# Sign convolutions with two output channels in one float32r weight, layer 1 by row pairs, and attention without the row maximum

## The chip, the core and the metric

The kernel runs on one core of a Trainium2 chip. Five engines work side by side and wait for one another through semaphores: TensorE (PE: matmuls, and PEld: the loads of their weights), VectorE (DVE), ScalarE (ACT), GpSimd (POOL) and SyncE (SP), which here only starts transfers. The metric is the device time of one execution in microseconds. Three runs of the kernel before gave 2253.57, 2254.1 and 2255.21 us; the profiled execution spans 2262.4 us.

## The reference

The input is 16 images of 256 channels and 28 x 28 pixels. Four layers follow each other.

- Layer 0: `sign(x)` is convolved (3x3, 256 to 256 channels) with `sign(w)`; the sum, times the mean of |w| per output channel, goes through a batch norm over all images and is added to x.
- Layer 1: `sign(x)` is convolved 3x3 with float32 weights clipped to -1..1; a fixed affine map, a parametric ReLU, a gate (two tiny dense layers on channel means, with ReLU and sigmoid), a product with the residual and another affine map follow. A second branch does the same with a 1x1 convolution.
- Layer 2: batch norm over all images, sign, sign convolution, parametric ReLU; batch norm, sign, sign convolution, parametric ReLU; batch norm, plus the input, parametric ReLU.
- Layer 3: attention over the 784 pixels of each image with 64 reduced channels:

```python
q = jnp.einsum('rc,bcn->bnr', Wq, xf)
k = jnp.einsum('rc,bcn->brn', Wk, xf)
v = jnp.einsum('rc,bcn->bnr', Wv, xf)
attn = jax.nn.softmax(jnp.einsum('bnr,brm->bnm', q, k) * scale, axis=-1)
out = jnp.einsum('cr,brn->bcn', Wp, jnp.einsum('bnm,bmr->brn', attn, v))
return out.reshape(B, C, H, W) + x
```

A batch norm over all images needs the statistics of every image before the next sign can be taken, so the work falls into stages: layer 0, layer 1, the first and the second convolution of layer 2, attention.

## The kernel before

Channels lie on the 128 partitions in two halves (`k` for input, `mo` for output), the 784 pixels of an image on the free axis. Each stage loops over the 16 images. A scheduler orders each engine's instructions from the program's order and the data dependencies; rotating buffers of the pools decide how far an image may run ahead.

A 3x3 convolution (`conv3x3`, L137) is 18 matmuls (two halves of input channels, nine taps) for each half of the output channels and each half image `h` (14 rows, 392 columns, one PSUM bank), accumulated in PSUM. Signs and sign weights are bfloat16: 72 matmuls an image for layer 0 (L243) and for each convolution of layer 2 (`conv2`, L441). In layer 1 the float32 weights are split into three bfloat16 parts (`split3`, L128), so the convolution takes 216 matmuls an image (L400, L418), and the 1x1 convolution (`conv1x1`, L364) 24.

Around the convolutions: in layer 0 ACT takes signs into a padded image (L212) and copies the integer sums to int16 tiles `y0` (L244), while DVE collects statistics (L246); y0, and later x2 in the same pool, stay in SBUF for all 16 images. In layer 1, `enter` (L297) makes x1, its signs and the residual; `bn_prelu` (L315) turns a PSUM sum into y; `gate_hidden` and `gate` compute the gates, and `branch1` and `branch2` (L350, L382) apply them one and two images later. In layer 2 `prelu_n` (L182) and the statistics (L448) are DVE's and the copy to int16 (L446) ACT's.

Attention works on chunks of 112 rows (`MC`), seven to an image. For each image `row_max` (L537) computes the scores chunk by chunk and reduces each to a row maximum on DVE; `put_max` (L550) transposes the maxima into an extra row of q, so that a second score product (`attend`, L569) comes out with the maximum subtracted; ACT takes the exponential (L574); another product with v sums the values, and, as 64 columns of v are ones, the denominators too (L581). DVE takes the reciprocal of the denominators (L586) and multiplies (L587). `project` (L590) multiplies with Wp and adds x. While image b is attended, `qkv(b + 1)` (L517) and `project(b - 1)` are put between its steps. All matmuls of attention are float32.

Of the kernel before, what the change touches and what calls it, by code (L numbers as in the profile page):

```python
"""conv_seq d4 on 16x256x28x28: binary conv + BN, two-branch SE block, binary conv x2 + BN, attention.

Layout: channels on partitions (two halves of 128), pixels (784) on the free axis, one tile per
image.  Activations that are signs (-1, 0, 1) and sign weights are held in bfloat16, and
convolution sums of signs (integers of magnitude <= 2304) in int16: both hold them exactly.  The
float32 weights that meet sign activations (layer 1) are split into three bfloat16 parts whose sum
is the float32 weight, so that these products are exact too; everything else is float32.

Algebra used: stop_gradient(a - b) + b is a; sums of 2304 signs never reach the saturation of layer
0; the mean of s*x + (1-s)*y is taken from the two means; a per-channel constant of layer 1's output  # L10
is carried along (`cc`) into layer 2's last bias, as layer 2's first batch norm doesn't see it.
"""
# [10 lines left out]
BF = mybir.dt.bfloat16  # L23
I16 = mybir.dt.int16
AF = mybir.ActivationFunctionType
# [7 lines left out]
N = S * S          # pixels of an image  # L33
HN = N // 2        # half an image: one matmul, one PSUM bank
HR = S // 2
K9 = 256 * 9
MC = 112           # attention rows per chunk
# [3 lines left out]
#: The per-channel vectors, in the order of their columns.  # L41
# [10 lines left out]
def conv_seq_kernel(ctx: ExitStack, tc: tile.TileContext, d: dict, out: bass.AP):  # L52
# [6 lines left out]
    xr = ctx.enter_context(tc.tile_pool(name="xr", bufs=B))  # L59

# [9 lines left out]

    pads = [const.tile([P, 2, S + 2, S + 2], BF, tag=f"pad{i}", name=f"pad{i}") for i in range(2)]
    for p in pads:
        nc.gpsimd.memset(p, 0.0)

# [7 lines left out]
    def inv_std(name, var):  # L82
        """1 / sqrt(var + EPS) of a [P, 2] tile, the square root's table corrected by a Newton step."""
        v, r, t = vtile(name + "_v"), vtile(name + "_r"), vtile(name + "_t")
        V.tensor_scalar(v, var, EPS, None, ALU.add)
        A.activation(t, v, AF.Sqrt)
        V.reciprocal(r, t)
        tt(t, r, r, ALU.mult)
        tt(t, t, v, ALU.mult)
        V.tensor_scalar(t, t, -0.5, 1.5, ALU.mult, ALU.add)  # L90
        return tt(r, r, t, ALU.mult)

    def affine(name, inv, gamma, beta, mean):
        """scale = gamma * inv and bias = beta - mean * scale."""
        s, c = vtile(name + "_s"), vtile(name + "_c")
        tt(s, gamma, inv, ALU.mult)
        tt(c, mean, s, ALU.mult)
        tt(c, beta, c, ALU.subtract)
        return s, c

# [1 line left out]
    def load_taps(pool, src, k, g):  # L102
        st = pool.tile([P, 3, 256], F32, tag="st", name="st", bufs=2)
        nc.sync.dma_start(out=st, in_=src[k, :, 3 * g:3 * g + 3, :])
        return st

    def sign_chunk(pool, dst, src, acc, k, g):
        """Three taps of sign(w) into dst, and their part of sum |w| in PSUM, [P, 2]."""
        st = load_taps(pool, src, k, g)
        A.activation(dst[:, k, 3 * g:3 * g + 3, :], st, AF.Sign)  # L110
        ab = pool.tile([P, 256], F32, tag="ab", name="ab", bufs=2)
        V.tensor_reduce(ab, st.rearrange("p t o -> p o t"), AX.X, ALU.add, apply_absolute_value=True)
        part = acc.tile([P, 2], F32, tag="sm", name="sumabs")
        for mo in range(2):
            T.matmul(part[:, mo:mo + 1], lhsT=ab[:, mo * P:(mo + 1) * P], rhs=ones, start=True, stop=True)
        return part

    def sign_weights(pool, dst, src, total, acc):
        """A list of steps: dst = sign(w), total = mean |w| per output channel."""
        def step(k, g):  # L120
            part = sign_chunk(pool, dst, src, acc, k, g)
# [4 lines left out]
        return [lambda k=k, g=g: step(k, g) for k in range(2) for g in range(3)]  # L126

    def split3(dsts, st):  # L128
        """clip(w, -1, 1) as the sum of three bfloat16 tiles."""
        V.tensor_scalar(st, st, -1.0, 1.0, ALU.max, ALU.min)  # L130
        A.copy(dsts[0], st)
        tt(st, st, dsts[0], ALU.subtract)
        A.copy(dsts[1], st)
        tt(st, st, dsts[1], ALU.subtract)
        A.copy(dsts[2], st)

    def conv3x3(ps, pad, wts, mo):  # L137
        """ps[:, h, :HN] = 3x3 convolution of the padded image, output channels of half mo."""
        n, last = 0, len(wts) * 18 - 1
        for w in wts:  # L140
            for k in range(2):
                for t in range(9):
                    r, c = divmod(t, 3)
                    for h in range(2):
                        T.matmul(  # L145
                            ps[:, h, :HN].rearrange("p (a b) -> p a b", b=S),
                            lhsT=w[:, k, t, mo * P:(mo + 1) * P],
                            rhs=pad[:, k, r + h * HR:r + h * HR + HR, c:c + S],
                            start=(n == 0),
                            stop=(n == last),  # L150
                        )
                    n += 1

    def inner(pad, k):
        return pad[:, k, 1:S + 1, 1:S + 1]
# [4 lines left out]
    def halves(ap):  # L160
        return ap.rearrange("p (h n) -> p h n", h=2)

    def mean_var(name, st):
        """Per-channel mean and variance from [P, 2, chunks, 6] statistics."""
# [8 lines left out]
    def sign_bn(name, sf, m, v, gamma, beta):  # L173
        """Batch norm of sf * n from the mean and variance of n: scale and bias for n."""
# [7 lines left out]
    def prelu_n(pool, n, alpha, bufs=2):  # L182
        """Parametric ReLU of the integers n (SBUF or PSUM, [P, 2, HN]) in float32."""
        t = pool.tile([P, 2, HN], F32, tag="t", name="t", bufs=bufs)
        p = pool.tile([P, 2, HN], F32, tag="p", name="p", bufs=bufs)
        V.tensor_scalar(t, n, 0.0, alpha, ALU.min, ALU.mult)  # L186
        V.scalar_tensor_tensor(p, n, 0.0, t, ALU.max, ALU.add)  # L187
        return p

    stats_x2 = const.tile([P, 2, 2 * B, 6], F32, name="stats_x2")  # L190
    stats = const.tile([P, 2, 2 * B, 6], F32, name="stats")
    sf0, sf1, sf2 = vtile("sf0"), vtile("sf1"), vtile("sf2")
    w0 = wpool.tile([P, 2, 9, 256], BF, tag="wa", name="w0")

    x2 = [None] * B
    with tc.tile_pool(name="ps_conv", bufs=3, space=PSUM) as psc, \
# [4 lines left out]

        with tc.tile_pool(name="ph1", bufs=1) as ph:
            # ======== layer 0: sign(x) * sign(w), kept as integers, with their statistics ========
            xs = [None] * B

            def load_x(b):
                xs[b] = ph.tile([P, 2, N], F32, tag="xs", name=f"xs{b}", bufs=3)
                nc.sync.dma_start(out=xs[b], in_=d["x"][b])

            def sign0(b):  # L210
                for k in range(2):
                    A.activation(inner(pads[b % 2], k), img(xs[b][:, k, :]), AF.Sign)  # L212

            steps = sign_weights(ph, w0, d["w0"], sf0, pss)
            load_x(0)
            sign0(0)
            for s in steps:
                s()
            load_x(1)

            w1 = [ph.tile([P, 2, 9, 256], BF, name=f"w1_{i}") for i in range(3)]
            fw = [ph.tile([P, 2, 256], BF, name=f"fw_{i}") for i in range(3)]

            def w1_step(k, g):
                st = load_taps(ph, d["w1"], k, g)
                split3([w[:, k, 3 * g:3 * g + 3, :] for w in w1], st)

            def fw_step():
                st = ph.tile([P, 3, 256], F32, tag="st", name="stf", bufs=2)
                nc.sync.dma_start(out=st[:, 0:2, :], in_=d["fw"])  # L230
                split3(fw, st[:, 0:2, :])

            steps = [lambda k=k, g=g: w1_step(k, g) for k in range(2) for g in range(3)] + [fw_step]
            y0 = [None] * B
            for b in range(B):
# [4 lines left out]
                y0[b] = xr.tile([P, 2, N], I16, tag="xr", name=f"y0_{b}")  # L240
                for mo in range(2):
                    ps = conv_ps()
                    conv3x3(ps, pads[b % 2], [w0], mo)  # L243
                    A.copy(halves(y0[b][:, mo, :]), ps[:, :, :HN])  # L244
                    for h in range(2):
                        V.bn_stats(stats[:, mo, 2 * b + h, :], ps[:, h, :HN])  # L246
                if b >= 2 and steps:
                    steps.pop(0)()
            load_x(0)
            load_x(1)  # L250

            # ======== layer 1 ========
            # Constants of the layer, [P, 2] each.
# [6 lines left out]
            def mix(name, scale, shift):  # L260
                """mean(s * (x + shift) + (1 - s) * y) = sum(x) * a + sum(y) * b + c."""
# [411 lines left out]
```

## Time and profile before

The page gives the busy time of each engine over the span of 2262.4 us, in which busy stretches of different engines overlap.

| what | value |
|---|---|
| time, median of three | 2254.1 us |
| TensorE busy | 2126.3 us, 94% |
| VectorE busy | 1041.2 us, 46% |
| ScalarE busy | 496.2 us, 22% |
| layer 0, first to last matmul | 12 to 209 us |
| layer 1 | 222 to 932 us |
| layer 2, first and second convolution | 933 to 1133 and 1143 to 1342 us |
| attention | 1358 to 2262 us |

A group of instructions is listed as line, engine, operation, output and input with their sizes, count; then busy time and mean duration of one; then the idle time of the engine just before them and what ended it. Matmuls are pipelined: the mean of one is longer than the distance between two. The granted clock is TensorE's, 1.0 being full.

### The profile page before, as it was taken

To read this page: it belongs to the slowest core of one execution; us is meant where nothing else is said; L and a number is where in the kernel's file an instruction comes from. 1 tells how busy PE (TensorE), PEld (TensorE's weight loads), DVE (VectorE), ACT (ScalarE), POOL (GpSimd) and SP (SyncE) were. 2 spreads that over 40 slices of the span, in tenths; PEclk is the share of its full clock that TensorE was granted. 3 is DMA by queue.
4 is the path that set the end of the run, shared out by engine and by line. 5 is a ranking of instruction groups with operands and counts; after the bars stand their busy time and mean duration, and the time that the engine had idled before them with its cause. 6 is when DMAs were issued, how large, how long until landed. Compare 5 with 4: busy or idle time off the path is not lost.

```text
span 2262.4 us, 22710 instructions
## 1 busy us (share of the span) xinstructions
PE 2126.3 (94%) x9896; PEld 1170.4 (52%) x9896; DVE 1041.2 (46%) x1628; ACT 496.2 (22%) x659; POOL 6.5 (0%) x13
## 2 busy tenths in 40 slices
PE   8998999999999998699989979999999999999997
PEld 4554555555555555355545544444444444444443
DVE  5213244454454454554567765677653233222232
ACT  5322122122122111323222321222211111111111
POOL 0000000000000000000000000000000000000000
PEclk9999999999999999799999985688778777777776
DMA  5221000000000000100000000000000000000000
GB/s 204 73 72 43 1 29 29 15 29 15 15 29 15 15 15 1 42 1 1 1 1 1 1 5 1 14 14 15 14 14 15 14 15 14 14 14 14 15 15 28
DMA packets 11603, 50.11 MB, mean 22 GB/s; under 512 B 1776, under 2 KB 2160, under 8 KB 11504
## 3 DMA queue, kind: packets, MB, share of 16 engines
q1 hardware_dynamic: 11504, 48.67, 6.2%
q8 instruction: 77, 1.26, 0.2%
q14 instruction: 22, 0.18, 0.0%
HBM read 35.82 MB, written 12.85 MB: 22 GB/s over the span
## 4 chain that ended last, share of the span: by engine, by line
PE 90%; DVE 8%; ACT 1%; issue 0%; DMA 0%; SPq 0%; ACTq 0%
PE cv L145 53%; PE sc L543 10%; PE sc L569 7%; PE av L581 6%; PE mi L594 4%; DVE r L586 4%; PE cv L372 3%; PE mi L522 3%; PE mi L531 2%; PE av L554 2%; PE gate L343 1%; DVE nm L547 1%; DVE p L187 1%; DVE x L515 0%; DVE t L186 0%; DVE x L511 0%
## 5 line engine op out<-in xcount | busy, mean ns | idle before, releaser
L145 PE MATMUL cv<-pad,w 128*128 128x392 bf16 x4608 | 799.4, 333 | 8.7 <-ACT pad L305 8.7
L145 PEld LDWEIGHTS <-w 128*128 128x128 bf16 x4608 | 445.0, 97 | 343.6 <-issue 12.2
L543 PE MATMUL sc<-qk 64*112 64x392 f32 x448 | 263.8, 764 | 51.6 <-DVE nm L547 51.6
L543 PEld LDWEIGHTS sc<-qk 64*112 64x112 f32 x448 | 116.3, 267 | 186.9 <-issue 116.9
L145 PE MATMUL cv<-pad,w2b 128*128 128x392 bf16 x1152 | 198.3, 334 | 11.1 <-ACT pad L465 11.1
L569 PE MATMUL sc<-qk 65*112 65x392 f32 x448 | 202.8, 575 | 0.0
L145 PE MATMUL cv<-pad,w2a 128*128 128x392 bf16 x1152 | 198.3, 333 | 2.4 <-ACT pad L436 2.4
L294 DVE TENSOR_SCALAR t<-sy,vec 128x784 f32<-128x784 f32 x32 | 20.1, 628 | 340.7 <-ACT sy L318 340.7
L581 PE MATMUL av<-es,va 112*128 112x392 f32 x448 | 170.2, 509 | 1.6 <-ACT es L574 1.6
L586 DVE RECIPROCAL r<-av 64x784 f32<-64x784 f32 x16 | 80.9, 5057 | 190.3 <-PE av L581 190.3
L547 DVE TENSOR_REDUCE nm<-sc 112x1 f32<-112x784 f32 x112 | 108.9, 972 | 121.2 <-PE sc L543 120.8
L145 PEld LDWEIGHTS <-w2b 128*128 128x128 bf16 x1152 | 111.9, 97 | 97.5 <-issue 13.6
L145 PEld LDWEIGHTS <-w2a 128*128 128x128 bf16 x1152 | 112.2, 98 | 87.3 <-issue 3.9
L186 DVE TENSOR_SCALAR t<-cv,vec 128x784 f32<-128x784 f32 x64 | 66.2, 1034 | 158.6 <-PE cv L145 158.6
L574 ACT ACTIVATE es<-sc 112x784 f32<-112x784 f32 x112 | 91.9, 823 | 205.3 <-PE sc L569 205.2
L569 PEld LDWEIGHTS sc<-qk 65*112 65x112 f32 x448 | 85.7, 202 | 82.9 <-issue 71.5
L581 PEld LDWEIGHTS av<-es,va 112*128 112x128 f32 x448 | 87.7, 196 | 69.4 <-issue 18.7
L446 ACT CAST n<-cv 128x784 int16<-128x784 f32 x64 | 52.0, 812 | 229.3 <-DVE p L187 229.3
L318 ACT ACTIVATE sy<-cv,abn_c,abn_s 128x784 f32<-128x784 f32 x32 | 32.1, 1003 | 315.4 <-PE cv L145 315.4
L594 PE MATMUL mi<-o,wp 64*128 64x392 f32 x128 | 88.3, 831 | 7.2 <-DVE o L587 6.2
L246 DVE BATCH_NORM_STATS2 stats<-cv 128x6 f32<-128x392 f32 x64 | 33.4, 564 | 125.8 <-ACT y L244 125.7
L522 PE MATMUL mi<-x,wqk 128*128 128x392 f32 x128 | 68.0, 688 | 14.3 <-DVE x L515 14.3
(182 smaller groups left out, 1536.9 us busy)
## 6 DMA issues: line engine op xcount, KB each, us to landing
xs<-in_x_dram SPq DMA_DIRECT2D x32, 784.0 KB, 4.3
out_dram<-x SPq DMA_DIRECT2D x16, 784.0 KB, 3.3
st<-in_w_dram SPq DMA_DIRECT2D x12, 384.0 KB, 3.9
st<-in_w2a_dram SPq DMA_DIRECT2D x6, 384.0 KB, 3.1
st<-in_w2b_dram SPq DMA_DIRECT2D x6, 384.0 KB, 3.2
stf<-in_fw_dram SPq DMA_DIRECT2D x1, 256.0 KB, 2.8
wqk<-in_wqk_dram SPq DMA_DIRECT2D x1, 128.0 KB, 2.1
wv<-in_wv_dram SPq DMA_DIRECT2D x1, 64.0 KB, 1.9
```

The lines of the kernel that those rows point to most:

```text
L145: T.matmul(ps[:, h, :HN].rearrange("p (a b) -> p a b", b=S), lhsT=w[:, k, t, mo * P:(mo + 1) * P], rhs=pad[:, k, r + h * HR:r + h * HR + H ...
L186: V.tensor_scalar(t, n, 0.0, alpha, ALU.min, ALU.mult)
L372: T.matmul(ps[:, h, :HN], lhsT=w[:, k, mo * P:(mo + 1) * P], rhs=z2[b][:, k, h * HN:(h + 1) * HN], start=(n == 0), stop=(n == 5),)
L446: A.copy(halves(nt[b][:, mo, :]), ps[:, :, :HN])
L522: T.matmul(ps[:, h, :HN], lhsT=wqk[:, k, :], rhs=x2[b][:, k, h * HN:(h + 1) * HN], start=(k == 0), stop=(k == 1),)
L543: T.matmul(ps[:MC, h, :HN], lhsT=q[0:64, c * MC:(c + 1) * MC], rhs=k_[0:64, h * HN:(h + 1) * HN], start=True, stop=True,)
L547: V.tensor_reduce(nm[:, c:c + 1], ps[:MC, :, :HN], AX.XY, ALU.max, negate=True)
L569: T.matmul(ps[:MC, h, :HN], lhsT=k_[:, c * MC:(c + 1) * MC], rhs=q[:, h * HN:(h + 1) * HN], start=True, stop=True,)
L574: A.activation(es[c], ps[:MC, :, :HN], AF.Exp, scale=0.125)
L581: T.matmul(av[:, h, :HN], lhsT=v_[:, c, :], rhs=es[c][:, h, :], start=(c == 0), stop=(c == NC_ - 1))
L586: V.reciprocal(r, av[64:P, :, :HN])
L594: T.matmul(ps[:, h, :HN], lhsT=wp[:, mo * P:(mo + 1) * P], rhs=o[:, h, :], start=True, stop=True)
```

## The change

It has three parts and some things that go with them.

First, sign convolutions (`sign_conv`). float32r is a 32-bit format for matmul operands of fewer significant bits than float32. Five of the six chunks of three taps (a chunk has one half of the input channels) get weights that hold two output channels at once: a + 4095 b, where a and b are signs of the channels o and o + 128. One matmul sums both; the sum over five chunks is A + 4095 B with |A| at most 1920, so rounding the sum over 4095 gives B: ACT adds 1.5 x 2^23 in float32, DVE takes it off again, and matmuls with -4095 and 1 times the identity take B out of the one PSUM sum and add it to the other. The sixth chunk is done plainly for both halves.

Second, layer 1 (`transform`, `conv`, `sum_pair`, `rows_out`). Two output rows are computed at once from four combinations of input rows and weight rows, so that 12 row products of a pair become 8; weights are split into two float32r parts. The 1x1 convolution uses two parts too.

Third, attention (`attend_unshifted`). The exponential is taken of the scores as they are. Queries and keys are split into a rounded and a remaining part, stacked on 128 rows, and a score chunk is two float32r matmuls for each half image. The value products of the two half images go to partitions 0 to 63 and 64 to 127 of one PSUM bank (columns of the array side by side), the projection takes the same rows of the array side by side. POOL adds the exponentials up; one product with ones gives the denominators, and normalization and projection of an image come during the next. Sums of the denominators and their reciprocals are kept; if they pass 1e18, a copy of the attention before (`attend_shifted`) is run afterwards.

With these go: layer 0's integers and x2 are stored to DRAM and loaded again, as the float32r tiles need the room; ReLUs move from DVE to ACT; the last three images of layer 1 are the first of layer 2; `keep_busy` puts matmuls whose result isn't used into the pauses between stages; layer 2 keeps its float32 activations `pt` instead of integers.

```diff
-    def conv3x3(ps, pad, wts, mo):
...
+    def sign_conv(pss, pad, w, temp):
...
+        for h in range(2):
+            for n in range(5):
+                for t in range(3):
+                    product(pss[0], h, w[0][:, n, t, :], n, t, n + t == 0, n + t == 6)
+            r, bs[h] = temp("t1"), temp("up", FR)
+            A.activation(r, pss[0][:, h, :HN], AF.Identity, bias=rounding, scale=1.0 / PACK)
+            V.tensor_scalar(bs[h], r, -ROUND, None, ALU.add)
+        for h in range(2):
+            for mo in range(2):
+                for t in range(3):
+                    product(pss[mo], h, w[1][:, t, mo * P:(mo + 1) * P], 5, t, mo == 1 and t == 0, False, mo == 0)
+        for h in range(2):
+            for mo in range(2):
+                T.matmul(
+                    pss[mo][:, h, :HN], lhsT=unpack[mo], rhs=bs[h], start=False, stop=True,
+                    skip_group_check=(mo == 0),
+                )
...
+            def transform(b):
...
+                terms = (
+                    (e0, e1, ALU.subtract), (o0, e1, ALU.add), (e1, o0, ALU.subtract), (o0, o1, ALU.subtract)
+                )
+                for pair in ((1, 2), (0, 3)):
+                    for k in range(2) if b == 0 else (slice(0, 2),):
+                        for u in pair:
+                            x, y, op = terms[u]
+                            tt(vs[b % 2][:, u, k], x[:, k], y[:, k], op)
...
+            def conv(b, mo, u, ps):
+
+                n = 0
+                for k in range(2):
+                    for w in w1:
+                        for c in range(3):
+                            T.matmul(
...
+            def sum_pair(b, mo):
...
+                A.activation(t1, ps[:, 0, :HN], AF.Identity, bias=c1[:, mo:mo + 1], scale=s1[:, mo:mo + 1])
+                V.scalar_tensor_tensor(up, ps[:, 1, :HN], s1[:, mo:mo + 1], t1, ALU.mult, ALU.add)
+                V.scalar_tensor_tensor(vp, ps[:, 1, :HN], ns1[:, mo:mo + 1], t1, ALU.mult, ALU.add)
...
+    def scores(b, c):
+        ps = two_banks(pssc, "sc")
+        for h in range(2):
+            for i in range(2):
+                T.matmul(
+                    ps[:MC, h, :HN], lhsT=ks[b][:, c * MC:(c + 1) * MC], rhs=qs[b][i][:, h, :],
+                    start=(i == 0), stop=(i == 1),
+                )
+        e = es[b, c] = buf("es", 5, shape=(MC, 2, HN))
+        A.activation(e, ps[:MC, :, :HN], AF.Exp, scale=0.125)
+        if c == 1:
+            sums[b] = buf("sum", 2, shape=(MC, 2, HN))
+            nc.gpsimd.tensor_tensor(sums[b], es[b, 0], e, ALU.add)
+        elif c > 1 and (b, c) != (B - 1, NC_ - 1):
+            nc.gpsimd.tensor_tensor(sums[b], sums[b], e, ALU.add)
+
+    def side_by_side(ps, w, e, start, stop):
+        for h in range(2):
+            T.matmul(ps[64 * h:64 * h + 64, :HN], lhsT=w, rhs=e[:, h, :], start=start, stop=stop)
...
+    again = nc.values_load(flag[0:1, 0:1], min_val=0, max_val=P)
+    with tc.If(again > 0):
+        attend_shifted(tc, d, out, wqk, wv, wp, va, pv, finish)
```

## The prediction

> **What bounds the kernel now.** I read the busy shares and the slices first, then the chain that ended last, then busy time by stage, then the groups.
>
> ```profile
> PE 2126.3 (94%) x9896; PEld 1170.4 (52%) x9896; DVE 1041.2 (46%) x1628; ACT 496.2 (22%) x659; POOL 6.5 (0%) x13
> PE   8998999999999998699989979999999999999997
> DVE  5213244454454454554567765677653233222232
> PEclk9999999999999999799999985688778777777776
> ```
>
> TensorE is busy in every slice; VectorE is nowhere near full. From slice 24 on, in the attention, the granted clock falls although TensorE stays busy.
>
> ```profile
> PE 90%; DVE 8%; ACT 1%; issue 0%; DMA 0%; SPq 0%; ACTq 0%
> PE cv L145 53%; PE sc L543 10%; PE sc L569 7%; PE av L581 6%; PE mi L594 4%; DVE r L586 4%; PE cv L372 3%; PE mi L522 3%; PE mi L531 2%; PE av L554 2%; PE gate L343 1%; DVE nm L547 1%; DVE p L187 1%; DVE x L515 0%; DVE t L186 0%; DVE x L511 0%
> ```
>
> The chain is TensorE nearly throughout; VectorE's 8% is mostly the reciprocal (L586), on the path once per image. So the number of matmuls and the columns per microsecond set the time. The columns of the next view are the stretch, its length, the busy time (and count) of PE, weight loads, DVE, ACT and POOL, granted clock, DMA share, GB/s:
>
> ```profile
> 12.00:209.00 197.00, 196.86 (x1158) 112.21 (x1157) 55.54 (x97) 66.16 (x84) 0.00 (x0) 1.00 0.28 93
> 274.00:892.00 618.00, 618.00 (x3735) 356.81 (x3733) 288.31 (x635) 126.38 (x203) 0.00 (x0) 1.00 0.06 19
> 933.00:1133.00 200.00, 198.69 (x1168) 113.43 (x1167) 99.09 (x137) 59.87 (x66) 0.74 (x1) 0.99 0.02 5
> 1143.00:1342.00 199.00, 198.16 (x1152) 111.73 (x1150) 136.51 (x186) 57.10 (x62) 0.94 (x2) 0.99 0.00 1
> 1400.00:2240.00 840.00, 786.85 (x2136) 407.04 (x2135) 354.91 (x330) 143.70 (x183) 0.00 (x0) 0.74 0.04 15
> 1755.90:1769.30 13.40, 13.40 (x21) 6.50 (x22) 5.57 (x6) 0.00 (x0) 0.00 (x0) 0.50 0.00 0
> ```
>
> Layer 0, layer 1 and the two convolutions of layer 2 are matmuls end to end (12.3, 42.6, 12.4, 12.4 us an image). Attention takes 55 us an image; the last row is one row_max pass: clock 0.50, matmuls all through it, right after TensorE waited 3.3 us for the reciprocal's queue.
>
> ```profile
> L145 PE MATMUL cv<-pad,w 128*128 128x392 bf16 x4608 | 799.4, 333 | 8.7 <-ACT pad L305 8.7
> L581 PE MATMUL av<-es,va 112*128 112x392 f32 x448 | 170.2, 509 | 1.6 <-ACT es L574 1.6
> L531 PE MATMUL mi<-wv,x 128*112 128x64 f32 x448 | 48.1, 266 | 2.0 <-DVE qk L527 2.0
> L531 PEld LDWEIGHTS mi<-wv,x 128*112 128x112 f32 x448 | 46.1, 180 | 11.3 <-DVE qk L527 11.0 <-DVE qk L559 0.2 <-issue 0.2
> L586 DVE RECIPROCAL r<-av 64x784 f32<-64x784 f32 x16 | 80.9, 5057 | 190.3 <-PE av L581 190.3
> L387 DVE SCALAR_TENSOR_TENSOR x<-su,g,x 128x784 f32<-128x784 f32 x32 | 31.6, 1029 | 0.1
> L389 DVE BATCH_NORM_STATS2 stats_x<-x 128x6 f32<-128x392 f32 x64 | 31.4, 553 | 0.0
> L318 ACT ACTIVATE sy<-cv,abn_c,abn_s 128x784 f32<-128x784 f32 x32 | 32.1, 1003 | 315.4 <-PE cv L145 315.4
> L446 ACT CAST n<-cv 128x784 int16<-128x784 f32 x64 | 52.0, 812 | 229.3 <-DVE p L187 229.3
> ```
>
> Mean durations of matmuls overlap, so I price a matmul by its spacing: 108 bf16 ones of 392 columns take 18.4 us on the chain, 0.171 each. A float32 product appears as two records; four records take 1.32 us at full clock, so a float32 matmul costs 0.66, four times bf16, and 1.34 at half clock (20 records in 13.4 us).
>
> **What the Trainium skill says.** (1) "TensorE: Matmul & The Clock Gate", Part 1: an idle window of some 3.4 us halves TensorE's clock. The trace agrees on the halving (3.3 us idle, then 0.50), but here it stays low for 20 to 30 us of busy float32 matmuls. (2) Same page, "Weight-path perf modes": the fast weight load is not used for float32. The trace agrees in sign: 178 ns at the median for 112 float32 columns (L531), 97 for 128 bf16. (3) "TensorEngine Tiling (Array Packing)", Key Properties: tiles work in parallel, and a change of tiling mode drains TensorE. Nothing before uses tiles side by side. (4) "GPSIMD Engine Reference", 3.1: a two-input float32 add of 2048 elements takes 4497 ns; POOL does none in the trace.
>
> **The change, part by part.**
>
> *The unknown price: a float32r matmul of 392 columns.* Low end 0.171 (one column a cycle, as bf16), high end 0.66 (as float32). I take 0.171: four times bf16 is what the four products of two operands split in halves cost, and the new code uses float32r only where one rounded half is enough (4095 a + b fits 12 bits; elsewhere the remainder is a second operand), so one product should be paid. Weight loads could bound it; but L531's records, each with its own 112-column float32 load, follow each other every 0.103 us (28 in 2.89), so 128 columns need some 0.118, under 0.171.
>
> *Sign convolutions (layer 0, layer 2 twice).* 72 bf16 matmuls an image become 30 packed, 12 plain and 4 unpacking: 46 x 0.171 = 7.9 us. Added on the way: per half, ACT rounds (L318's 1003 ns at 784 elements less 392 x 0.81, the slope between copies of 448 and 784 elements at 532 and 805 ns: 0.68) and DVE subtracts (0.4; a float32 tensor_scalar of 512 took 419 ns). Between the last packed matmul and the unpacking that needs it stand about ten others (1.7 us), about the length of that chain with two hand-overs, so I add 0.4: 8.3 an image. In layer 0 the preparation of w1 gives DVE up to 3.5 us more in an image, 6.6 in all, still under 8.3. In layer 2 DVE has 0.8 + 2 x 0.97 + 4 x 0.56 = 5.0 us, ACT 2 x 1.04 + 2 x 0.68 + 2 x 0.82 = 5.1: hidden. Integers of layer 0 and x2 go through DRAM: 1.2 MB per 8 us is 150 GB/s, against 246 that the first 12 us moved. Each stage: 16 x 8.3 = 133.
>
> *Layer 1.* 216 bf16 matmuls an image become 2 x 4 x 12 = 96 float32r ones (16.4 us), the 1x1 convolution 16 for 24 (2.7), gates 1: TensorE 20. VectorE an image: enter 2.2, transform four adds of 840 elements (955 ns at 768, so 1.03 each) 4.1, residual 2.1, sum_pair and rows_out 8 of 392 elements at 0.6 (1.03 an element: 955 ns at 768, 692 at 512), prelu_out, unit_b and branch1_b 2 x 1.1 each, branch2 2 x 1.03 + 4 x 0.55 = 4.3, small ones 0.6: 24.5. ACT: 2 x 0.95 for each of signs, residual, z2; 2.7 for sum_pair and rows_out, 2.0 for branch1_a, 4.0 for unit_a, 1.5 for gates: 16. So VectorE takes over as the bound. Its queue is in order and waits on ACT and PSUM at several places (behind sum_pair's wait for ACT stand the next image's transform, and behind that TensorE): 5% for that, 26 an image, 416. TensorE's waits for vs are shorter than the 3 us that cost it the clock. The transform is bounded by 2.1 (if two bf16 elements go per cycle) and 4.1.
>
> *Attention.* Gone: row_max (14 float32 matmuls, 18.7 at the low clock), put_max (2.7), the 5.0 reciprocal from the path. TensorE an image: scores 28 float32r (4.7), queries and keys 4 float32 (2.7), project_v as before (2.9), values 14 float32 of 64 output rows in column pairs (9.3 one after the other, 4.7 if pairs run together), denominators 1.3 or 0.7, projection in row pairs 2.7 or 1.3: 23.6 or 17.0. I take pairs running together plus 3 us for some twenty mode changes and waits: 20; the ends are 17 and 26.5. ACT: 7 exp (5.8), copies 3.4, batch norm and relu 3.7, the two sums for the limit 1.2: 14. VectorE 12 (reciprocal of 392 columns at 6.45 ns: 2.5). POOL: six adds of 784, at the page's 2.2 ns an element 1.7 each (estimate), 10.3; even if VectorE's two-input work (4.6) excludes it, 15. The exp of a chunk waits for a buffer of es that POOL still reads; behind it on ACT stand the copies of queries and keys, and behind those TensorE, but five buffers are over half an image of slack. All below 20: 320.
>
> *Float32 fallback.* attend_shifted runs only if sums pass 1e18. Evaluated on the reference's inputs, the scaled scores stay below 20 and all sums total 2e9: it costs only the test, taken as 5.
>
> *Boundaries.* Before: 13 (209 to 222), 40 (892 to 932), 10, 16. They keep their chains of statistics and small vector work; layer 1's tail loses one third of a 1x1 convolution but gains gates in common: 14, 32, 8, 15. Start 14, end of attention (pipeline fill and last projection) 15.
>
> *Sum.* 14 + 133 + 14 + 416 + 32 + 133 + 8 + 133 + 15 + 320 + 15 + 5 = 1238 of span; the profiled span before is 8 over the timed 2254, so **1230 us**.
>
> **Rivals.** (a) *Pairs do not run together, and queues jam:* attention 25.5 an image (+88) and layer 1 at 28 (+32): 1350. For it: float32 records come in twos for the same columns and start in order; against: only neighbours of different columns need to overlap. (b) *float32r needs two cycles a column (0.33):* moving data is twice as wide as bf16. Sign convolutions 15.4 an image (x48 = 739), layer 1 becomes TensorE's again at 38.5 (616), attention 24.7 to 26 (410), boundaries 103: 1870. Against: the two-cycle float32 records do two products. (c) *As slow as float32 (0.66), the other side:* 46 x 0.66 x 48 = 1460, layer 1 75 x 16 = 1200, attention 33 x 16 = 530, boundaries 103: 3290, slower than before. Against: the rounding would then be pointless. (d) *A low clock in the attention,* as now: PE 20 becomes up to 34, +220: 1450. For it: row_max shows how long it lasts; against: no 3 us of idle is left in the loop, as the reciprocal is taken off the path by one image of delay.
>
> **How the numbers follow.** Forecast 0.68, (a) 0.13, (b) 0.07, (c) 0.03, (d) 0.09. The low end 1120: transform at 2.1 (-32), attention 17 (-48), layer 0 and 2 at 7.9 (-19), and a little more hiding. The high end 1420 takes in (a) and most of a half (d). Outside: (b), (c), part of (d), some of each tail: 0.2. Slower: (c) and a thousandth of the rest, 0.03; no change within 0.2% only by accident, 0.01; faster 0.96.
>
> **What would show it.** float32r matmuls spaced 0.171 us (0.33 or 0.66 means b or c). Layer 1 at about 26 us an image with VectorE over 90% busy and TensorE near 77%, waiting on vs. Layer 0 and 2 at 8 to 8.5 an image with TensorE over 93%. Attention at 20 with clock near 1.0, neighbouring value matmuls starting together; at 26 they do not. No instruction of attend_shifted. The forecast fails if the float32r spacing is off, if VectorE's rows get longer with these operand types, or if POOL's adds take much over 2 us and hold the es buffers.

## The result, and the profile after

The changed kernel takes 1260.3 us (median of four runs, 1257.2 to 1261.1) where the kernel before takes 2254.7 in the same session: a ratio of 0.5587, with a 95% interval of 0.5579 to 0.5595. The forecast was 1230, in a range of 1120 to 1420. The profiled execution has a span of 1254.7 us.

The page's busy shares and slices, in the form in which they were shown for the kernel before:

```profile
PE 1157.3 (92%) x5936; PEld 971.8 (77%) x5940; DVE 823.4 (66%) x1420; ACT 705.1 (56%) x1050; POOL 220.4 (18%) x165
PE   5999989999999999966978989999889999999996
DVE  5563269989999999864544554454577657576644
PEclk9999999999999999977998998999979999999998
```

TensorE is still busy in nearly every slice, but VectorE now has a stretch at 8 and 9 tenths of its own, slices 7 to 17: that is layer 1. The clock row is the second thing to see: the attention, the last quarter, is granted full clock, where before its slices had 0.5 to 0.8. The chain that ended last, by engine:

```profile
PE 78%; DVE 12%; ACT 7%; issue 1%; DMA 1%; POOL 1%; SPq 0%; ACTq 0%; POOLq 0%; DVEq 0%
```

TensorE's share of it has gone from 90% to 78%, VectorE's from 8% to 12%, ScalarE's from 1% to 7%: waits on other engines that were beside the path are now on it. Busy time by stage, with the columns of the stage table shown for the kernel before (layer 0; layer 1; the two convolutions of layer 2; attention):

```profile
20.30:168.80 148.50, 147.16 (x740) 138.44 (x740) 64.65 (x150) 76.83 (x120) 8.56 (x15) 1.00 0.42 149
179.60:558.00 378.40, 357.70 (x1924) 347.65 (x1924) 343.45 (x633) 238.55 (x356) 16.55 (x29) 0.99 0.21 73
581.00:745.00 164.00, 151.17 (x754) 141.60 (x755) 77.48 (x141) 75.17 (x101) 0.00 (x0) 0.96 0.27 93
758.60:903.00 144.40, 144.28 (x729) 134.06 (x728) 67.92 (x122) 70.58 (x94) 0.00 (x0) 1.00 0.00 1
927.00:1235.00 308.00, 306.45 (x1587) 179.29 (x1587) 196.13 (x161) 200.65 (x301) 179.86 (x94) 0.99 0.18 66
```

Two rows are not full: layer 1, where TensorE has 21 us free, and the first convolution of layer 2, 13 us, though the second, the same work, has none. Against the forecast's sum:

| stage | forecast, us | after, us | difference |
|---|---|---|---|
| start | 14 | 20.3 | +6 |
| layer 0 | 133 | 148.5 | +16 |
| to layer 1 | 14 | 10.8 | -3 |
| layer 1 | 416 | 378.4 | -38 |
| its tail, to layer 2 | 32 | 23.0 | -9 |
| layer 2, first convolution | 133 | 164.0 | +31 |
| between | 8 | 13.6 | +6 |
| layer 2, second convolution | 133 | 144.4 | +11 |
| to the attention | 15 | 24.0 | +9 |
| attention | 320 | 308.0 | -12 |
| its end, and the test for the fallback | 20 | 19.7 | 0 |
| span | 1238 | 1254.7 | +17 |

The other 14 of the 30 us between 1230 and 1260.3 come from the step from span to time: before, the profiled span was 8 longer than the timed median; after, it is 6 shorter. So the sum is right to 17 us, but of terms that are wrong by up to 38 in both directions. Four of them need a cause: the sign convolutions (too short), layer 1 (too long), the first convolution of layer 2 (much too short), and the attention, which came out right and might have done so by accident.

The means of matmuls overlap again (0.35 us on the page for L197 and L467), and their spacing is read below. GpSimd's sum takes 1.93 us (1.7 was forecast), the rounding L209 0.59 (0.68) and the reciprocal of 392 columns 2.6 (2.5). No instruction of `attend_shifted` is in the trace.

### The profile page after: what moved, and what is told of

It is laid out like the page before. It is cut to its first block, busy times and chain, and to the rows that moved or that the text cites. A ratio compares the mean times of both kernels' runs of the same rounds, so it can differ in the third digit from the quotient of the medians.

```text
span 1254.7 us, 15446 instructions
## 1 busy us (share of the span) xinstructions
PE 1157.3 (92%) x5936; PEld 971.8 (77%) x5940; DVE 823.4 (66%) x1420; ACT 705.1 (56%) x1050; POOL 220.4 (18%) x165
## 4 chain that ended last, share of the span: by engine, by line
PE 78%; DVE 12%; ACT 7%; issue 1%; DMA 1%; POOL 1%; SPq 0%; ACTq 0%; POOLq 0%; DVEq 0%
PE cv L197 31%; PE cv L467 14%; PE sc L879 7%; PE av L893 7%; PE sm L925 4%; PE mi L860 3%; PE cv L217 2%; PE mi L935 2%; DVE x L596 1%; PE unused L287 1%; ACT y L542 1%; DVE x L551 1%; DVE stats L598 1%; ACT rn L427 1%; PE cv L564 1%
## 5 line engine op out<-in xcount | busy, mean ns | idle before, releaser
L467 PE MATMUL cv<-vs,w 128*128 128x392 f32 x1536 | 301.6, 354 | 8.4 <-DVE y L500 7.2
L197 PE MATMUL cv<-fpad,wpk 128*128 128x392 f32 x1440 | 302.6, 358 | 0.8 <-DVE wpk L158 0.8
L467 PEld LDWEIGHTS cv<-vs,w 128*128 128x128 f32 x1536 | 286.2, 190 | 12.7 <-DVE y L500 10.0
L197 PEld LDWEIGHTS cv<-fpad,wpk 128*128 128x128 f32 x1440 | 272.1, 193 | 11.5 <-ACT t L209 7.6
L889 POOL TENSOR_TENSOR sum<-sum,es 112x784 f32<-112x784 f32 x79 | 152.6, 1931 | 40.8 <-ACT es L884 35.8
L197 PE MATMUL cv<-fpad,wpl 128*128 128x392 f32 x576 | 139.5, 370 | 13.7 <-DVE p L710 9.7
L209 ACT ACTIVATE t<-cv,rounding 128x392 f32<-128x392 f32 x96 | 56.4, 588 | 168.9 <-PE cv L197 165.5
L197 PEld LDWEIGHTS cv<-fpad,wpl 128*128 128x128 f32 x576 | 106.0, 195 | 32.1 <-ACT t L209 17.4
L879 PEld LDWEIGHTS sc<-q,kt 128*112 128x112 f32 x448 | 72.3, 176 | 57.8 <-issue 35.8
L879 PE MATMUL sc<-q,kt 128*112 128x392 f32 x448 | 109.1, 366 | 1.6 <-ACT es L884 1.2
L893 PE MATMUL av<-es,va 112*64 112x392 f32 x448 | 100.8, 508 | 0.0
L564 PE MATMUL cv<-z,fw 128*128 128x392 f32 x256 | 51.5, 351 | 5.1 <-ACT z L555 5.0
```

The lines of the kernel that those rows point to most:

```text
L197: T.matmul(ps[:, h, :HN].rearrange("p (a b) -> p a b", b=S), lhsT=lhsT, rhs=pad[:, k, r + h * HR:r + h * HR + HR, c:c + S], start=start, s ...
L209: A.activation(r, pss[0][:, h, :HN], AF.Identity, bias=rounding, scale=1.0 / PACK)
L467: T.matmul(ps.rearrange("p (a b) -> p a b", b=S), lhsT=w[:, k, c, u, mo * P:(mo + 1) * P], rhs=vs[b % 2][:, u, k, :, c:c + S], start=(n == 0),
L564: T.matmul(ps[:, h, :HN], lhsT=w[:, k, mo * P:(mo + 1) * P], rhs=z2[b][:, k, h * HN:(h + 1) * HN], start=(n == 0), stop=(n == 3),)
L879: T.matmul(ps[:MC, h, :HN], lhsT=ks[b][:, c * MC:(c + 1) * MC], rhs=qs[b][i][:, h, :], start=(i == 0), stop=(i == 1),)
L889: nc.gpsimd.tensor_tensor(sums[b], sums[b], e, ALU.add)
```

## The experiments

Theory 1 is the forecast's, corrected where the trace already shows it: float32r streams its columns in one pass, TensorE sets the sign convolutions and the attention, VectorE's queue sets layer 1. Its rivals: the float32r weight load or the wider data costs more than was taken (sign convolutions); TensorE sets layer 1 as well; the attention is set by waits and not by side-by-side products.

**Prices of matmuls alone (m1_matmul_prices).** The kernel runs nothing but groups of 40 matmuls on tiles in SBUF, each group of another type, width or pattern:

```python
for i in range(40):
    T.matmul(ps[:, 0:392], lhsT=wf[:, i % 8, :], rhs=xf[:, 0:392], start=(i == 0), stop=(i == 39))
```

> The kernel leaves out all four layers: it loads one image, makes bf16, float32r and float32 copies of it and runs groups of 40 equal matmuls back to back, then stores the image 16 times. It measures what sets the spacing of float32r matmuls, 0.19 us in the changed kernel where 0.171 was forecast. Theory A, the weight load sets it (128 four-byte columns need about 0.187 us, about 1.46 ns each): float32r with 128 weight columns is spaced 0.187 at 256 and at 392 moving columns alike and about 0.215 at 512; 112 weight columns give about 0.165 to 0.17, 64 give about 0.165. Theory B, the wider moving data set it (0.48 ns a column): 256 columns 0.124, 512 columns 0.245, and the number of weight columns makes no difference. For both, bf16 is spaced 0.166 to 0.171. Side question, float32 products of 64 output rows: 0.327 a record in the same columns, about 0.17 a record when they alternate between the two column halves.

The timeline of TensorE, as start, length, engine, line, operation, tiles and shapes. The price of one is the distance from one start to the next row's start, over 40:

```profile
19.83 6.80 PE L97 MATMUL ps<-xb,wb 128*128 128x392 bf16 x40
26.46 7.33 PE L100 MATMUL ps<-xb,wb 128*128 128x392 bf16 x40
35.83 7.28 PE L106 MATMUL ps<-xf,wf 128*128 128x392 f32 x40
42.95 7.63 PE L109 MATMUL ps<-xf,wf 128*128 128x392 f32 x40
50.42 9.49 PE L112 MATMUL ps<-xf,wf 128*128 128x512 f32 x40
59.75 4.91 PE L115 MATMUL ps<-xf,wf 128*128 128x256 f32 x40
64.50 7.36 PE L118 MATMUL ps<-xf,wf 128*112 128x392 f32 x40
```

bfloat16 at 392 columns (L97): 6.63 / 40 = 0.166 us. float32r at 392 (L106): 0.178; at 512 (L112): 0.233; at 256 (L115): 0.119. That is 0.445 ns a column (0.114 for 256 more), 6 to 7% above bfloat16's 0.42, and no floor from the weight load: a new 128-column load every 0.119 us is kept up. Loading 112 weight columns for 128 changes nothing (L118: 0.180), nor does using the same weights again (0.176, in a group further down). So the weight-load theory falls, and spacing does grow with the columns moved, as the other theory has it, with a smaller size than its 0.48; that the width of the data is the reason is not shown. Reading 14 rows of 28 out of rows of 30, as a convolution does, costs 0.009 more for float32r (L109: 0.187) and 0.013 for bfloat16 (L100: 0.179). The group has one such pattern only: in the kernel before, bfloat16 spacings in a convolution lie between 0.165 and 0.180, 0.171 on average. In the changed kernel the rows of a convolution stand at 0.190 from start to start; here are 14 in layer 2, and the next record starts at 807.35:

```profile
804.69 2.82 PE L197 MATMUL cv<-fpad,wpk 128*128 128x392 f32 x14
```

L467 has the same (47 in 8.99 us), and contiguous columns stand at 0.18 (L217 and L564). So the kernel adds 0.003 at most to the price of the pattern alone. Further groups of this run price float32: a product costs two records of 0.331, 0.66 in all, and two products in different column halves take 0.171 a record, half of the 0.326 of products in the same half.

**Another ring for the staged weights (e1_stage_buffers).** In the first convolution of layer 2 the images come 12.9 to 14.0 us apart for five images and 9.1 later. The timeline of this stretch, issue of the weights for the next convolution first; its last row has the columns of the stage table, for the 3.3 us from 647.3:

```profile
645.85 0.38 SPq L135 DMA_DIRECT2D st<-in_w2b_dram  x1
647.24 2.33 PE L197 MATMUL cv<-fpad,wpl 128*128 128x392 f32 x6 [2.36 <-DVE p L710]
650.99 0.84 ACT L157 ACTIVATE sg<-st 128x768 bf16<-128x768 f32 x1 [4.16 <-DMA st<-in_w2b_dram]
651.74 0.57 ACT L209 ACTIVATE t<-cv,rounding 128x392 f32<-128x392 f32 x1
...
647.30:650.60 3.30, 3.30 (x10) 3.30 (x11) 2.71 (x5) 0.00 (x0) 0.00 (x0) 0.50 0.77 313
```

The weights (`st`) go into a ring of three buffers under the tag "r", which the ReLU outputs (L709) share. So their transfer starts only when a ReLU tile is free, half an image late; ScalarE then waits 4.16 us for it at L157, in the middle of its queue, and the rounding L209 of the image stands behind that. Behind the rounding stand the unpacking, the ReLU and VectorE's p, and TensorE waits for PSUM that p frees (2.36 us before 647.24). Three of the four waits of this length are followed by 3.4 us at half clock, in which these six matmuls take 2.33 us, where the same six of the image before (at 642.91) take 1.42: part of the price is the clock. The edit gives them a ring of their own:

```diff
-            steps = [rest[1]] + both(*sign_weights(ph, w2b, d["w2b"], sf2, pss, ("r", 3)))
+            steps = [rest[1]] + both(*sign_weights(ph, w2b, d["w2b"], sf2, pss, ("st", 2)))
```

> The weights of layer 2's second convolution are staged in two buffers of their own instead of taking turns with the r tiles of the first convolution's ReLU. Theory A, the shared buffers cause the 13.9 us images of the first convolution (load, sign, sum, ReLU and PSUM in one ring): all its images take about 9.1 us, the stage falls from 164 to about 145, the time from 1260 to about 1238. Rival, DVE and ACT work for the weights is simply too much in these images: 1260 within 5.

Measured: 1243.1 us (1241.1 to 1244.6), ratio to before 0.549 (0.547 to 0.552). The images of the stage come every 7.7 to 10.6 us, every 9.1 in the end, and the second convolution begins at 744 instead of 758. About 4 us are given back earlier: layer 2's first matmul comes at 585 instead of 581. A wait of 1.5 us of VectorE for the first transfer of these weights, which now falls into that boundary, is part of this; the rest was there before the boundary and has no cause here. The shared ring was the cause of the long images, and its price is 14 us between the two profiled spans (1254.7 and 1240.9) and 17 between the medians of time.

**The parts undone, one at a time (e2_plain_sign_convs, e3_shifted_attention).** e2 puts back 72 bfloat16 matmuls for a sign convolution; e3 calls the attention of before at once.

```diff
-    attend_unshifted(tc, d, out, wqk, wv, wp, va, worst, pv, finish)
...
-    with tc.If(again > 0):
-        attend_shifted(tc, d, out, wqk, wv, wp, va, pv, finish)
+    attend_shifted(tc, d, out, wqk, wv, wp, va, pv, finish)
```

> The first part of the change alone is undone: sign convolutions are 72 bf16 matmuls an image again, without packing and rounding; layer 1 and attention stay changed (one staging buffer of the sums of weights is dropped for room). If the packing is worth what its matmuls say, 72 x 0.171 = 12.3 us an image against 9.1, less the staging stalls of 19 us that hide in longer images: 3 x 16 x 3.2 - 19 = 135 more, 1395. If packing were eaten by its waits and rounding, under 1300.

> The third part alone is undone: attention with row maximum and float32 scores as before, layers 0 to 2 as changed. Expected from the stage of before: 905 us against 352 from the end of the second convolution, so about 1260 + 550 = 1810. Rival: the stage before was slowed by its clock, which may be better behind another stage; if the clock alone recovers, 16 x 15 less, 1570.

Measured: e2 1388.3 us (ratio 0.614, 0.611 to 0.617), e3 1832.5 (0.810, 0.806 to 0.814; its granted clock is 0.853 over the span, 0.967 in the changed kernel). The rival for e3, that the old attention only needed a better clock (1570), falls. So the packed signs are worth 128 us, with the wait of e1 still in the changed kernel, and the attention 572, its clock included. Of the whole 994 there remain, by difference, 294 for layer 1 and what goes with it; no run undoes that part.

**Which engine sets layer 1 (e4_half_conv, e5_less_vector).** The two take work from one engine each.

```diff
-                    for w in w1:
+                    for w in w1[:1]:
...
-                                stop=(n == 11),
+                                stop=(n == 5),
```

> Layer 1's convolution without the low part of its weights: 6 of the 12 matmuls of each row product, 48 fewer in an image (leaves the low part out). 48 x 0.195 us = 9.4 us of TensorE less in an image. Theory A (TensorE at 22.4 and VectorE at 22.0 us of a 23.4 us image bound layer 1 together): VectorE takes over at once, an image at 22.2 to 22.8, -10 to -20 in all: 1240 to 1250. Theory B (TensorE alone is the bound, VectorE has slack): up to -9 an image, about 1110 to 1150. Theory C, the forecast's (VectorE alone): nothing beyond the boundary and first image, 1250 to 1260.

```diff
-                    V.scalar_tensor_tensor(x, r, ra1[:, k:k + 1], x, ALU.mult, ALU.add)
+                    if k == 0:
+                        V.scalar_tensor_tensor(x, r, ra1[:, k:k + 1], x, ALU.mult, ALU.add)
...
-                    for i in range(2):
-                        V.bn_stats(stats[:, k, 2 * b + i, :], v[:, i * HN:(i + 1) * HN])
+                    if b % 4 == 0:
+                        for i in range(2):
+                            V.bn_stats(stats[:, k, 2 * b + i, :], v[:, i * HN:(i + 1) * HN])
```

> Layer 1 with less VectorE work: statistics of x2 only for every fourth image, and the residual's scalar_tensor_tensor for one channel half only (leaves out three quarters of those statistics and half of the residual's PReLU). VectorE loses 1.0 + 0.75 x 4 x 0.49 = 2.4 us in an image. Theory A (bound together): TensorE's 22.4 stays, -0.6 to -1.0 an image: 1244 to 1251. Theory C (VectorE alone, the forecast's): -2.4 an image, 1222. Theory B (TensorE alone): 1260.

Measured: e4 1257.6 us (ratio 0.5566, 0.5547 to 0.5585), e5 1245.8 (0.5512, 0.5493 to 0.5530). One image's length of layer 1 of the changed kernel, of e4 and of e5, in the columns of the stage table:

```profile
408.10:431.50 23.40, 22.41 (x120) 21.70 (x120) 21.82 (x41) 14.76 (x23) 0.53 (x1) 1.00 0.24 87
```

```profile
408.10:431.50 23.40, 16.96 (x73) 15.93 (x73) 22.43 (x41) 15.37 (x24) 0.53 (x1) 0.79 0.26 91
```

```profile
408.10:431.50 23.40, 23.40 (x130) 23.30 (x130) 22.21 (x42) 14.76 (x22) 0.53 (x1) 1.00 0.26 87
```

In e4 TensorE loses 48 matmuls of an image, and the images still come every 23.7 us (mean of nine; 23.6 in the changed kernel over the same nine, 23.4 from the eighth on): TensorE alone does not set them. In e5 TensorE is full (23.40 of 23.40) and the same nine images come every 22.4 us: with VectorE relieved by 2.4, TensorE takes over after 1.2. So VectorE's queue, its waits included, sets layer 1, and TensorE stands a little over 1 us behind it. My reading before the two runs, that both set it together, was right for e5 and wrong for e4, where it had asked for 22.2 to 22.8. The changed kernel's VectorE queue over one image shows why 22 us of work make 23.4:

```profile
412.80 1.03 DVE L110 TENSOR_TENSOR vs<-pad 128x840 fp32r<-128x840 bf16 x1
413.75 0.62 DVE L489 SCALAR_TENSOR_TENSOR up<-cv,abn_s,t 128x392 f32<-128x392 f32 x1
...
415.91 1.98 DVE L110 TENSOR_TENSOR vs<-pad 128x840 fp32r<-128x840 bf16 x2
419.42 0.17 DVE L110 TENSOR_TENSOR gates<-gates,s 128x4 f32<-128x4 f32 x1 [1.54 <-ACT gates L534]
```

Two things stand in it. An instruction starts 0.08 us before the one ahead of it ends (1.03 at 412.80, the next at 413.75), so the sum of durations overstates the queue. And the one gap of the image, 1.5 us, is the wait for the gates (ScalarE's sigmoid L534, behind TensorE's two small products and a ReLU). Nothing else in the image leaves VectorE free. e4 has a lesson of its own, in TensorE's timeline:

```profile
420.28 4.65 PE L564 MATMUL cv<-z,fw 128*128 128x392 f32 x16 [3.36 <-ACT z L555]
```

After an idle time of 3.36 us the 16 matmuls of L564 take 4.65 us where they took 3.03 (another gap, of 3.08, stands before L467), and the mean clock is 0.79 in this image and 0.80 in the stage. Work taken off an engine that is not the bound came back as a lower clock.

**The value products (e6_value_order, e8_one_half).** e6 changes only the order in a group of four products, from left, right, left, right half of the columns to left, left, right, right. e8 sends most of the second half image's products to the left half too.

```diff
-        side_by_side(avs[b], va[b % 2][:, c, 0:64], es[b, c], c == 0, c == NC_ - 1)
+        w = va[b % 2][:, c, 0:64]
+        if c == 0:
+            side_by_side(avs[b], w, es[b, c], True, False)
+        else:
+            for h in range(2):
+                T.matmul(avs[b][:64, :HN], lhsT=w, rhs=es[b, c][:, h, :], start=False, stop=c == NC_ - 1 and h == 1)
...
```

> Attention's value products reordered: for two chunks first the two of columns 0 to 63, then the two of columns 64 to 127; the same instructions, but only every second neighbour is in the other half of the array. Theory A (neighbours in different column halves run at the same time, 0.171 us a record where one after the other are 0.327): a group of 8 records goes from 4 pairs at a time to about half of that; +0.3 to +0.7 us a pair of chunks, +1.2 to +2.8 an image if TensorE is the bound: 1280 to 1305. Theory B (they gain nothing here, the 20 us of an image come from ScalarE and GpSimd waits): 1258 to 1264.

> Value products of the second half image go to columns 0 to 63 as well (leaves the second half's sum out, but for its first and last chunk), so that nothing lies beside them: 13 products in a row in place of 7 pairs in an image. Theory A (halves run at the same time, and TensorE sets the attention): 6 x 0.65 = 3.9 us more in an image, 16 images: about 1320 (1305 to 1330). Theory B (ScalarE, VectorE or GpSimd sets it): 1258 to 1275. Theory C (there was no overlap to lose): 1260.

Measured: e6 1258.7 us (ratio 0.5569, 0.5551 to 0.5587), e8 1310.6 (0.5791, 0.5752 to 0.5829). TensorE's timeline around one group, of the changed kernel, of e8 and of e6, where the next record starts at 1014.45; two records make a product:

```profile
1013.30 1.54 PE L893 MATMUL av<-es,va 112*64 112x392 f32 x8
1014.67 0.83 PE L893 MATMUL sm<-sum,ones 112*64 112x392 f32 x4
```

```profile
1008.74 2.85 PE L905 MATMUL av<-es,va 112*64 112x392 f32 x8
1011.51 1.69 PE L879 MATMUL sc<-q,kt 128*112 128x392 f32 x8
```

```profile
1013.08 1.54 PE L974 MATMUL av<-es,va 112*64 112x392 f32 x8
```

Eight records take 1.37 us side by side and 2.77 in one half. An image of the attention comes every 22.9 us in e8, 19.9 in the changed kernel: 3.0 of the 3.9 that six more products in a row would cost on a TensorE without slack. So the overlap is real, it is worth some 50 us, and TensorE sets the attention to within 0.9 us an image. e6 could not tell this: the products stand in the new order in the built program, and still its records start two by two and the group of eight takes 1.37 us as well. So two products in the same half may stand next to each other without loss as long as the other half has its products two places on. Its expectation rested on the wrong picture, that only direct neighbours overlap.

**GpSimd's sums (e9_two_sums) and GpSimd's help in layer 1 (e7_pool_term).** e9 leaves four of the six sums of an image out; e7 is e1 with one of the four transform terms moved from VectorE to GpSimd.

```diff
-        elif c > 1 and (b, c) != (B - 1, NC_ - 1):
+        elif c == 2:
```

```diff
-                            tt(vs[b % 2][:, u, k], x[:, k], y[:, k], op)
+                            eng = V if b == 0 or u != 3 else nc.gpsimd
+                            eng.tensor_tensor(vs[b % 2][:, u, k], x[:, k], y[:, k], op)
```

> GpSimd adds the exponentials of three of the seven chunks only (leaves the others out of the denominators): four adds of 1.9 us fewer in an image. If GpSimd's adds hold the buffers of the exponentials, or stretch VectorE's rows where TensorE waits for them, the attention gets shorter by 1 to 3 us in an image: 1210 to 1245. If TensorE sets it: 1256 to 1261, with VectorE's two-input rows back at 1.0 us from 1.70.

> With the staging buffers of the run before (e1_stage_buffers, 1243) and one of the four transform terms of layer 1 on GpSimd from the second image on: VectorE loses 1.03 us in an image, GpSimd gains about 3.6 (1680 elements at 2.1 ns, two channel halves). Theory A (VectorE and TensorE bound layer 1 together): -0.3 to -0.8 an image, 1231 to 1239. Rival (GpSimd's two-input add shuts VectorE's two-input work out while it runs, as beside the sums of attention, 1.70 for 0.98 us): VectorE's rows stretch by as much as it is relieved or more, 1243 to 1270.

Measured: e9 1256.1 us (ratio 0.5547, 0.5510 to 0.5584, which overlaps the changed kernel's), images every 19.9 us as before. A sum of GpSimd and VectorE's addition of x (L838) beside it in the changed kernel, then the group of these additions in e9 (busy time, mean ns of one, idle time before):

```profile
1041.20 2.13 POOL L889 TENSOR_TENSOR sum<-sum,es 112x784 f32<-112x784 f32 x1
1041.54 2.62 DVE L838 TENSOR_TENSOR x<-p,x 128x784 f32<-128x784 f32 x1
```

```profile
L838 DVE TENSOR_TENSOR x<-p,x 128x784 f32<-128x784 f32 x22 | 20.4, 968 | 0.0
```

The first of an image's two additions starts while the sum runs and takes 2.62 us, 1.79 of them beside it; the second, with no sum beside it, takes 0.96, so a mean over both, 1.86, mixes two different things. The additions for q and kt (L871, L869), whose one input lies in PSUM, take 0.97 us with a sum beside them nearly all the time. The long one costs nothing, as VectorE has time to spare there. e7: 1240.0 us (ratio 0.5484, 0.5466 to 0.5502), against e1's 0.5494 (0.5467 to 0.5521): not to be told apart. VectorE falls from 21.8 to 20.9 us an image and the same nine images come every 23.4, for 23.6. The expectation's rival does not show: the rows that stand beside GpSimd's term, with an input in PSUM or one input alone, keep their 0.62 and 0.56 us. VectorE now waits for the convolution at `rows_out` (6.9 us in five images) and TensorE for VectorE's `y` in turn (2.8): the loop of PSUM tiles between the two may set it, but no run tried a deeper one, so this stays open. It also limits what e5 shows: less work for VectorE shortens an image only where its waits don't grow by as much. e1 and e7 are the fastest versions measured.

## Why the prediction was right, and where it was not

**What bounds it, and the fates of the rivals: right.** *float32r in one pass* held: 0.178 against the 0.33 of rival (b) and the 0.66 of (c). *Pairs run together* held (0.171 a record, e8), so (a) falls. *The clock recovers* held (1.00 and 0.99 in all steady stages but the first convolution of layer 2, 0.96), so (d) falls. The prediction took 3 us of idle time for the danger, and less is enough: "TensorE: Matmul & The Clock Gate", Part 1, of the Trainium skill gives some 3.4 us for the idle window; e4 has lost the clock after gaps of 3.1 and 3.4, and the first convolution of layer 2 in the changed kernel after gaps of 2.4. Why a float32r product is one pass was argued from products of split operands; the runs show the price, not this reason.

**Sign convolutions: mechanism right, the spacing mis-sized.** The step took 0.171 for a float32r matmul, bfloat16's spacing, from the argument that one rounded product should be paid. It is 0.190 in this kernel's pattern. 42 x 0.190 + 4 x 0.18 = 8.7, and the images of the second convolution come every 9.1: the 0.4 us allowed for waits are there, as four pauses of some 0.09 in an image, and the price of a matmul is what was short. 0.8 us too little, 48 images: 40 of the +58 of the three stages. ScalarE and VectorE are hidden as said (70.6 and 67.9 of 144.4). That weight loads would not bind held: 256 columns pass at 0.119, each with a new load.

**The first convolution of layer 2: a wait not foreseen.** The prediction costed the preparation of w1 in layer 0 as work and the staged weights of layer 2 not at all. What it missed is in the code, a shared tag and so a shared ring, and not in the profile of before. 14 to 17 us (e1).

**Layer 1: mechanism right, VectorE's term mis-sized.** Forecast: 24.5 of work and 5% of waits, 26. Measured: 22.0 and 6%, 23.4. The rows of the transform cost what was said (1.03), and it does not run at two elements a cycle. But the step added durations up; 28 long instructions that each overlap the next by 0.08 are 2.2 of the 2.5 us that were too many. The Trainium skill has it in "Vector Engine (DVE) Microarchitecture Reference", 5.2 "Measured stream behaviour on trn2": 1.0417 ns a column and about 75 ns of fixed cost after queue overlap. That makes an estimate of 0.95 us for 840 columns, and the queue above shows 0.95 from start to start; for 784 columns it makes 0.89, where the same queue shows 0.95 again (the two rows of L596 in 1.89). TensorE came to 22.4 and not 20, mostly by the spacing, and was busy for 95% of the stage where 77% was forecast, so that a forecast with both terms right would have had VectorE ahead by 1 us only. TensorE waits, where it does, not for the transform as said but for PSUM that VectorE frees at L500 (6.2 us in five images).

**Attention: right, for the stated reasons as far as the trace shows.** 19.9 an image against 20, of 17 to 26.5. From start to start in the trace: scores 6.1, values 6.0, v 2.7, queries and keys 2.5, projection 1.7, denominators 0.8, 19.8 in all. The forecast's terms without waits were 4.7, 4.7, 2.9, 2.7, 1.3 and 0.7, 17.0; the 3 us added for mode changes and waits are found mostly in the first two, and they are mode changes. Scores between two groups of value products, in the changed kernel:

```profile
995.54 1.69 PE L879 MATMUL sc<-q,kt 128*112 128x392 f32 x8
```

The next group starts at 997.16. The eight take 1.62 us, where eight at their spacing of 0.18 take 1.44. From record to record the loss sits at the changes alone: the last matmul before a change takes 0.1 us longer and the first after it 0.06 to 0.11. An image has 13 changes, not twenty, and they add 2.5 us. The sums on GpSimd, 1.93 for the estimate of 1.7, hold nothing up (e9).

**Boundaries.** Forecast 103 with the start and the end, measured 111. The start (+6) and the step to the attention (+9) were not taken apart.

**The step from span to time** carried the 8 us of before over, and 14 us of the miss are that. It had the wrong sign: in every timed execution on record the time is 1.7 to 3.1 us above the span of the same execution. The profiled execution of the kernel before, 2262.4, was a longer one than the three timed; the span of 1238 was a forecast of about 1240.

**Luck.** That the total came within 30 us owes much to terms that cancel: layer 1 was 38 too long and the three sign convolutions 58 too short.

## What to carry to other kernels

Price a VectorE queue from start to start in the timeline, not by adding durations: here that is 0.95 for 1.03 and moved the forecast of a stage by some 36 us. Before costing staged transfers at nothing, look at whose ring of buffers they use: one tag shared with the activations put a transfer in the middle of ScalarE's queue and cost some 15 us. And when two engines stand within 1 us of each other, take work from each in turn to see which one binds; relief of either is soon given back. Where matmuls of different tilings alternate, count the changes: here each cost some 0.2 us.

## What the runs showed of the hardware that was not expected

- float32r is about a quarter of float32's cost at 392 columns (0.178 and 0.66), and 7% above bfloat16; neither the number of weight columns (64, 112, 128) nor a new load for each matmul changes it.
- Two float32 products in the same column half next to each other lose nothing if products for the other half follow (e6, eight records in 1.37 us in both orders).
- A change between the whole array and tiles side by side costs TensorE some 0.2 us, half before it and half after it: 13 changes in an image of the attention add 2.5 us.
- A VectorE add of two float32 tiles in SBUF that starts beside a GpSimd add takes 2.62 us instead of 0.96, as if it waited for the 1.79 that are left of that add; adds with one input in PSUM keep their 0.97.
- With 48 of the some 120 matmuls of an image gone, TensorE ran layer 1 at a clock of 0.80, with waits of 2 to 4 us in it. In the first convolution of layer 2 three of four waits of 2.4 us were followed by 3.4 us at half clock.
